# A four-layer graph network in one list schedule: the planner gets the SBUF port of VectorE and GpSimd as a resource, finer costs, and new ranks

## The chip, the cores and the metric

The kernel runs on one core of a Trainium2 chip. The metric is the device time of one execution in microseconds (us), and the figure for a kernel is the median over its runs. The engines are called by the names of the profile: PE (TensorE), DVE (VectorE), ACT (ScalarE), POOL (GpSimd) and SP (SyncE, which here only issues DMAs). PEld is PE's weight load.

## The reference

The input `x` holds 128 batches of 128 nodes by 512 features, all in f32; `adj` is one 128x128 matrix. Four layers follow each other, and each is `x = layernorm(x + layer(x))`:

```
layer 0:  y = adj @ x[b];  y @ weight + bias
layer 1:  h = x @ W;  e = leaky_relu(s1[:,None] + s2[None,:]) * adj   (s1, s2 = h @ a1, h @ a2)
          elu(softmax(e) @ h + beta * h)
layer 2:  A = adj @ x,  C = adj @ x + b;  max over nodes of relu(A + (C - A))
layer 3:  8-head attention masked where adj == 0, projection,  o + layernorm(o) * gamma + beta
```

Batches are independent of each other. The order of the work is free as long as each batch goes through its layers in turn.

## The kernel before

**Tiling.** A batch is one 128x512 tile. Batches are taken in groups: 31 groups of four and, at the end, two groups of two (`PAIRS`). Layer 0 and layer 1 multiply two batches at a time, layer 3's Q, K and V a group at a time. These products use a scheme with seven block multiplications where the plain one has eight (`seven`, `pair_product`, `section`). The scheme needs four differences of activation blocks for each product (`differences`, line 908, on POOL) and, once, sums of weight blocks (`sums`, line 587, on POOL). The first `DIRECT` batches go through layer 0 with the plain product instead (`product`, line 362, and `mixed`, line 370). A batch that is not direct is mixed by line 389, transposed by DVE (line 392), and reordered through a scratch tensor in DRAM.

**Storage.** All activations live in one SBUF arena of 105 units, cut into classes of slots (`CAPS`, `SIZES`). PSUM has eight banks. Activations that wait for the end of layer 3 are spilled to DRAM and fetched again, except for the last `KEPT` batches.

**The order.** Nothing orders the engines but the order in which instructions are issued on each of them, and semaphores between them. That order is made when the program is built, by a list scheduler, the class `Plan`. Every batch, group and side task is a Python generator (a chain). It yields requests such as `use("DVE", 0.7, "t")`: engine, planned duration in us, slots that it needs. `Plan.at` gives the earliest time at which a request can start by the plan's own clock; `Plan.run` always takes the request with the earliest start, then the smaller order (`follow`, `urgent`, other), then the smaller rank, and lets its chain emit the instructions. A planned duration is multiplied by a factor for its engine (`SLACK`: DVE 1.05, ACT 1.1, POOL 1.0, SP 1.1), and the time from the end to the next step is `HANDOFF`, or, for a DMA, its own figure times `LATE`. The plan's times only decide the order. On the chip, every instruction starts when its engine and its semaphores let it.

In the plan before, one request often covers several DVE instructions. The three passes at lines 733, 737 and 739 and the reduction at 745 are one request of 2.2 us, lines 1415 and 1419 are one of 2.0 us, and the two passes of line 1151 are one of 1.7 us.

**Ranks.** A batch's rank is its number (the last 20 get four less, `early`). Constants shift it: `SECTION` for Q, K and V, `PROJ` for what follows attention, `SOFT` for the softmax, `SOON` for each of the last six groups, `SUMS0` and `SUMS3` for the weight sums. `RUN` makes a batch wait until the group that many groups earlier has its layer-3 input. `tiled` weaves the score matmuls (line 1049) of a group with the attention products (line 1070) of the one before it; for the last `APART` groups the attention products are chains of their own (`attend`). For the last `WHOLE` batches the softmax of layer 3 is taken whole (lines 1252 to 1258: an addition on DVE, one exponential on ACT, a sum on DVE); for the others, ACT takes eight exponentials with their row sums (line 1262).

**Lines that the steps touch.** DVE with two inputs in SBUF: 733, 737, 739, 757 (layer 1's attention), 1151 (its logits), 1175 and 1192 (elu), 1270 (softmax scale), 1415 and 1419 (layer 3's norm). DVE with an input in PSUM: 800, 804, 806, 818 (sums of the seven products), 1143, 1240. POOL: 309 (the power -0.5 of a variance), 355 (`pool_add`), 587, 908. ACT: 343 to 349 (layer norm), 812 (copies out of PSUM), 1311.

Of the kernel before, what the change touches and what calls it, by code (L numbers as in the profile page):

```python
# [18 lines left out]
G = 4  # L19
APART = 7  # L20
FIRST = 0
PAIRS = 2
SOON = (-2, 0, -2, 6, 12, 18)
WHOLE = 4
KEPT = 7
ATTENDS = 2
RUN = 7
SEVEN0 = 1
SUMS2 = 1
SUMS0 = 2  # L30
SUMS3 = 12
# [4 lines left out]
PLAIN = 4  # L36
GUESTS = 12
STICK = 0.4
CLOSE = 2900
SOFT = 4  # L40
PROJ = -5
SECTION = 14
PACE = 0
# [14 lines left out]
LAST, AHEAD = 20, 4  # L58
DIRECT = 12
LATER = 3  # L60
LANDED = 2.2
LATE = 1.3
HANDOFF = {"PE": 0.2, "DVE": 0.13, "ACT": 0.16, "POOL": 0.09, "SP": 0.05}
DVE_ = 1.05
ACT_ = 1.1
POOL_ = 1.0
SP_ = 1.1
SLACK = {"PE": 1.0, "DVE": DVE_, "ACT": ACT_, "POOL": POOL_, "SP": SP_}
BORDERS = 0.1
MARGIN = 0.5  # L70
LAND, ROW_LAND = 2.8, 0.0053
# [13 lines left out]
class Plan:  # L85
# [16 lines left out]

    def use(self, engine, work, take=None, late=None, urgent=False, follow=False, kind=""):
# [7 lines left out]
        return engine, work * SLACK[engine], names, late, 0 if follow else 1 if urgent else 2, kind  # L111

# [48 lines left out]
    def at(self, r):  # L161
        engine, _, take, _, order, _ = r["want"]
        spare = MARGIN if r["ready"] < CLOSE else 0.7
        early = min(spare, r["ready"] / 20) if engine == "PE" and order else 0.0
        t = max(r["ready"] + early, self.free.get(engine, 0.0))
        names = take()
        wanted = {}
        for name in names:
            n = SIZES.get(name, 0)
            wanted[n] = wanted.get(n, 0) + 1  # L170
        for n, count in wanted.items():
            free = self.blocks[n] if n else self.banks
            t = max(t, min(free) if count == 1 else sorted(free)[count - 1])
        for name in set(names) & set(CAPS):
            t = max(t, sorted(self.caps[name])[names.count(name) - 1])
        return t
# [29 lines left out]
    def run(self):  # L206
        while self.requests:
            t, _, _, n = min(
                (self.at(r) + self.border(r["want"]), r["want"][4], r["rank"], n)
                for n, r in enumerate(self.requests)  # L210
            )
            assert t < float("inf"), "the chains wait for each other"
            r = self.requests.pop(n)
            t = self.at(r)
            engine, work, take, late, _, kind = r["want"]
            if engine == "PE":
                work += BORDERS * (kind != self.kind)
                self.kind = kind
            self.free[engine] = t + work
            self.now = r["ready"] = t + work + late  # L220
            got = self.claim(take(), t)
            self.step(r, got[0] if len(got) == 1 else got)

# [8 lines left out]
def gnn_stack_kernel(  # L232
# [74 lines left out]
    def root(ve, rstd, follow=False):  # L307
        yield use("POOL", 0.62, urgent=True, follow=follow)
        nc.gpsimd.tensor_tensor(rstd, ve, neghalf, op=ALU.pow)  # L309
        return rstd  # L310
# [39 lines left out]

    def pool_add(dst, other, event, after=None, work=1.38):
        if after:
            yield after
        yield use("POOL", work)
        nc.gpsimd.tensor_tensor(dst, dst, other, op=ALU.add)  # L355
        done(event)
# [223 lines left out]
    def sums(s):  # L580

        for out, a, b, op in (
            (S1, S3, A22, ALU.add), (S2, S1, A11, ALU.subtract),
            (S3, A11, S3, ALU.subtract), (S4, A12, S2, ALU.subtract),
        ):
            yield use("POOL", 1.4)
            nc.gpsimd.tensor_tensor(weight(s, out), weight(s, a), weight(s, b), op=op)
# [26 lines left out]
    def logit_rows(a_sb, slot):  # L614

        yield w1_in
        wa = const.tile([P, K, 2], F32, name="wa")
        for s in range(2):
            for k in range(K):
                b_s = yield use("DVE", 0.7, "t")  # L620
# [88 lines left out]
    def attention1(gr, h):  # L709
# [21 lines left out]
        )  # L731
        be = yield use("DVE", 2.2, "u", urgent=True)
        nc.vector.tensor_tensor(
            z, z, s[:, 2 * h : 2 * h + 2, 0:1].to_broadcast([P, 2, P]), op=ALU.add
        )
        e = buf(be, 2, P)
        nc.vector.scalar_tensor_tensor(e, z, ALPHA, z, op0=ALU.mult, op1=ALU.max)
        give(bz)
        nc.vector.tensor_tensor(
            e, e, adj_cols.rearrange("p c r -> p (c r)")[:, None, :].to_broadcast([P, 2, P]),  # L740
            op=ALU.mult,
        )
        n = small.tile([P, 3, 2], F32, name="logits", bufs=4)
        nmx, sums, rs = n[:, 0], n[:, 1], n[:, 2]
        nc.vector.tensor_reduce(nmx, e, axis=AX.X, op=ALU.max, negate=True)
        yield use("ACT", 0.77)
        for i in range(2):
# [3 lines left out]
            )  # L751
        bt = yield use("DVE", 1.6, "u")
        nc.vector.reciprocal(rs, sums)
        et = buf(bt, Q, 2, S)
        for i in range(2):

            nc.vector.scalar_tensor_tensor(
                e[:, i, :], e[:, i, :], rs[:, i : i + 1], beta_id, op0=ALU.mult, op1=ALU.add
            )
            nc.vector.transpose(et[:, :, i, :], e[:, i, :].rearrange("p (c r) -> p c r", c=Q))  # L760
# [12 lines left out]
    def gather(gr):  # L773
# [16 lines left out]
        gr.xT[2] = buf(gr.slot["xT", 2], 1, 2, n)  # L790
        yield from differences(gr.block, gr.have, gr.used, 0.18 + 0.58 * gr.half, gr.first)

# [106 lines left out]
    def differences(blocks, have, used, time, rank):  # L899

        for out, a, b, when, t in (
            (T3, B22, B12, None, T3), (T1, B12, B11, None, T1),
            (B11, B22, T1, used[B11], T2), (B21, B21, B11, used[B21], T4),
        ):
            if when:
                yield when
            yield use("POOL", time, urgent=True)
            nc.gpsimd.tensor_tensor(blocks(out), blocks(a), blocks(b), op=ALU.subtract)  # L908
            done(have[t])

    def pair_product(rank, s, ready, blocks, release, out, finished, differed=None, into=None):
# [23 lines left out]

        plan.start(differences(blocks, have, used, 0.78, rank), rank)

# [161 lines left out]
    def batch(i):  # L1099
# [47 lines left out]
        yield wa_ready  # L1147
        b_s = yield use("DVE", 1.7, "t")
        unread = buf(b_s, D)
        for j in range(2):  # L1150
            nc.vector.scalar_tensor_tensor(  # L1151
                unread, xb, 1.0, wa_rows[:, j, :], op0=ALU.mult, op1=ALU.mult,
# [7 lines left out]
        if SEVEN1:  # L1160
# [12 lines left out]
            unread = be  # L1173
            yield use("DVE", 0.75, urgent=True)
            nc.vector.scalar_tensor_tensor(xb, ex, 0.0, xb, op0=ALU.max, op1=ALU.add)
            yield use("ACT", 0.52, urgent=True)
            nc.scalar.activation(ex, ex, AF.Exp)
        else:
# [10 lines left out]
            unread = bp  # L1189
        yield use("DVE", 0.77)  # L1190
        total = row_sums()
# [58 lines left out]
        if i >= NB - WHOLE:  # L1250
            yield use("DVE", 1.4)
            nc.vector.tensor_tensor(
# [6 lines left out]
        else:  # L1259
            for j in range(H):  # L1260
# [4 lines left out]
                )  # L1265
        yield use("DVE", 0.1 if SCALED == H else 0.1 + 1.45 * (1 - SCALED / H))
        rs = small.tile([P, H], F32, name="rs3")
# [139 lines left out]
    def normed(i, o, release, fetched):  # L1407
# [20 lines left out]
    def last(i, oT, v, release, biased):  # L1428
# [22 lines left out]
        for h, columns in enumerate(halves):  # L1451
# [7 lines left out]
            give(bp)  # L1459
            plan.start(pool_add(xb[:, columns], o[:, columns], added, biased, 0.9), i)  # L1460
        yield use("DVE", 0.32, follow=True)
# [3 lines left out]
        rooted, _ = beside(root(ve, rstd, follow=True), i)  # L1465
        b_t1 = yield use("DVE", 0.66, "t", follow=True)
        t1 = buf(b_t1, D)
# [4 lines left out]
        yield added  # L1472
        yield use("DVE", 1.8, follow=True)
        nc.vector.scalar_tensor_tensor(xb, t1, rstd, xb, op0=ALU.mult, op1=ALU.add)
# [54 lines left out]
```

## Time and profile before

| | us |
|---|---|
| median of 3 runs | 2994.31 |
| lowest and highest | 2992.17, 2995.53 |
| the profiled execution | 2995.11 |
| its span, first to last instruction | 2993.1 |
| PE busy | 2941.6 |
| DVE busy | 2457.0 |
| ACT busy | 2402.7 |
| POOL busy | 1873.3 |

The mean granted PE clock over the span is 0.996. Durations in what follows come from the profiled execution, whose own time lies 0.8 us above the median. "Busy" is the time in which an engine has an instruction in flight. A view of groups gives, for each line and shape, the count, the summed busy time and the mean duration, and the idle time of the engine just ahead of them with what ended it. A view of waits gives the waiting engine and line, the engine and line that it waited for, then the sum, the number of waits and the longest.

### The profile page before, as it was taken

What the parts mean: (1) busy time and instruction counts of PE and PEld (TensorE: products, weight loads), DVE (VectorE), ACT (ScalarE), POOL (GpSimd) and SP (SyncE); (2) the same over time, 40 slices, a digit from 0 to 9 for tenths busy, and PEclk for the clock granted to TensorE, in tenths of its full rate; (3) what the DMA queues carried; (4) which work ended last, traced back from release to release, by engine and by line L of the source; (5) the groups of instructions that cost most, each with busy time, mean ns of one, the idle gap of its engine ahead of it and who ended that gap; (6) DMA issues with size and microseconds to landing.
All of it is one profiled execution on the core that took longest, in us unless ns stands there. A gap on an engine that the chain in (4) does not pass through costs nothing. (4 is left out here: it accounts for less than half of the span.)

```text
span 2993.1 us, 55166 instructions
## 1 busy us (share of the span) xinstructions
PE 2941.6 (98%) x16503; PEld 2481.8 (83%) x16503; DVE 2457.0 (82%) x5775; ACT 2402.7 (80%) x7368; POOL 1873.3 (63%) x2049
## 2 busy tenths in 40 slices
PE   8999999999999999999999999999999999999997
PEld 5788788888888888888888888888888888888886
DVE  7977888877888888888878788887898877878778
ACT  4789688787978888888787887887888878778885
POOL 7954657555656756565755676665676647565555
PEclk9999999999999999999999999999999999999999
DMA  6535546544655655554654646555655545454443
GB/s 208 137 88 148 160 130 164 141 129 115 179 140 148 164 141 156 149 151 128 163 138 113 184 135 162 147 140 135 166 152 144 156 134 153 114 140 124 116 141 127
DMA packets 884105, 430.84 MB, mean 144 GB/s; under 512 B 572128, under 2 KB 785760, under 8 KB 883808
## 3 DMA queue, kind: packets, MB, share of 16 engines
q1 hardware_dynamic: 865376, 393.75, 48.7%
q10 hardware_dynamic: 18432, 33.56, 3.0%
q8 instruction: 133, 2.18, 0.3%
q14 instruction: 164, 1.34, 0.1%
HBM read 222.36 MB, written 204.80 MB: 143 GB/s over the span
## 5 line engine op out<-in xcount | busy, mean ns | idle before, releaser
L908 POOL TENSOR_TENSOR arena<-arena 128x256 f32<-128x256 f32 (+1 forms) x868 | 763.0, 888 | 325.1 <-PE ps L921 82.3
L309 POOL TENSOR_TENSOR sums<-sums,neghalf 128x1 f32<-128x1 f32 x511 | 322.4, 633 | 511.5 <-ACT sums L345 504.5
L921 PE MATMUL ps<-wsum_sb,arena 128*128 128x256 f32 x2208 | 547.1, 381 | 13.5 <-POOL arena L908 8.0
L921 PEld LDWEIGHTS ps<-wsum_sb,arena 128*128 128x128 f32 x2208 | 415.6, 191 | 95.3 <-POOL arena L908 14.7
L921 PE MATMUL ps<-w_sb,arena 128*128 128x256 f32 x1952 | 482.2, 381 | 5.0 <-DVE arena L806 3.5
L970 PE MATMUL ps<-arena,wqkv_sb 128*128 128x256 f32 (+1 forms) x2112 | 480.8, 373 | 0.0
L812 ACT COPY arena<-ps 128x256 f32<-128x256 f32 (+1 forms) x892 | 338.3, 395 | 158.7 <-PE ps L921 91.0
L970 PEld LDWEIGHTS ps<-arena,wqkv_sb 128*128 128x128 f32 x2112 | 393.5, 191 | 67.3 <-issue 16.2
L343 ACT ACTIVATE arena<-arena,sums 128x512 f32<-128x512 f32 x499 | 357.0, 716 | 114.5 <-DVE sums L338 94.1
L921 PEld LDWEIGHTS ps<-w_sb,arena 128*128 128x128 f32 x1952 | 371.0, 191 | 79.9 <-issue 20.2
L349 ACT ACTIVATE arena<-arena,sums 128x512 f32<-128x512 f32 x511 | 415.9, 814 | 17.1
L806 DVE TENSOR_TENSOR arena<-ps,arena 128x256 f32<-128x256 f32 (+1 forms) x669 | 291.7, 452 | 133.5 <-ACT arena L812 57.0
L1262 ACT ACTIVATE arena<-arena,nmx 128x128 f32<-128x128 f32 x992 | 388.3, 394 | 10.2 <-DVE nmx L1248 10.2
L970 PE MATMUL ps<-arena,wsum_sb 128*128 128x256 f32 (+1 forms) x1584 | 356.6, 374 | 5.6 <-POOL arena L908 3.7
L970 PEld LDWEIGHTS ps<-arena,wsum_sb 128*128 128x128 f32 x1584 | 293.8, 191 | 57.6 <-issue 11.0
L1276 ACT ACTIVATE arena<-arena,rs 128x128 f32<-128x128 f32 x768 | 281.1, 395 | 12.4 <-DVE rs L1268 8.2
L355 POOL TENSOR_TENSOR arena<-arena,beta_sb 128x512 f32<-128x512 f32 x128 | 170.3, 1334 | 141.3 <-DVE arena L1223 130.1
L1151 DVE SCALAR_TENSOR_TENSOR arena<-arena,wa_rows 128x512 f32<-128x512 f32 x256 | 224.7, 879 | 21.7 <-ACT arena L349 17.0
L970 PE MATMUL ps<-wqkv_sb,arena 128*128 128x256 f32 x1024 | 242.0, 380 | 0.0
L921 PE MATMUL ps<-wproj_sb,arena 128*128 128x256 f32 x992 | 240.5, 384 | 0.2
L970 PEld LDWEIGHTS ps<-wqkv_sb,arena 128*128 128x128 f32 x1024 | 194.4, 190 | 31.5 <-issue 4.7
L355 POOL TENSOR_TENSOR arena<-arena,bproj_sb 128x512 f32<-128x512 f32 x124 | 173.8, 1411 | 65.1 <-ACT arena L812 54.2
(120 smaller groups left out, 5490.9 us busy)
## 6 DMA issues: line engine op xcount, KB each, us to landing
p_d<-arena SPq DMA_DIRECT2D x256, 256.0 KB
arena<-p_d SPq DMA_DIRECT2D x128, 512.0 KB
x_d<-arena SPq DMA_DIRECT2D x244, 256.0 KB
arena<-x_d SPq DMA_DIRECT2D x976, 64.0 KB
arena<-in_x SPq DMA_DIRECT2D x127, 256.0 KB
out<-arena ACTq DMA_DIRECT2D x127, 256.0 KB
x_s<-arena SPq DMA_DIRECT2D x121, 256.0 KB
arena<-x_s SPq DMA_DIRECT2D x121, 256.0 KB
```

The lines of the kernel that those rows point to most:

```text
L309: nc.gpsimd.tensor_tensor(rstd, ve, neghalf, op=ALU.pow)
L343: nc.scalar.activation(buf_or_bank(unread), xb, AF.Square, bias=nm, accum_out=squares)
L349: nc.scalar.activation(xb, xb, AF.Identity, bias=nmr, scale=rstd)
L355: nc.gpsimd.tensor_tensor(dst, dst, other, op=ALU.add)
L806: nc.vector.tensor_tensor(c, a, c, op=ALU.add)
L812: nc.scalar.copy(c, a)
L908: nc.gpsimd.tensor_tensor(blocks(out), blocks(a), blocks(b), op=ALU.subtract)
L921: nc.tensor.matmul(p, t[:, k], w[:, k, :], start=first and k == 0, stop=final and k == 1, skip_group_check=True,)
L970: nc.tensor.matmul(to, lhs, rhs, start=first and j == 0 and k == 0, stop=final and k == 1, skip_group_check=True,)
L1151: nc.vector.scalar_tensor_tensor(unread, xb, 1.0, wa_rows[:, j, :], op0=ALU.mult, op1=ALU.mult, accum_out=gr.s[:, b, j : j + 1],)
L1262: nc.scalar.activation(pr[:, j, :], pr[:, j, :], AF.Exp, bias=nmx[:, j : j + 1], accum_out=sums[:, j : j + 1],)
L1276: nc.scalar.activation(pr[:, j, :], pr[:, j, :], AF.Identity, scale=rs[:, j : j + 1])
```

## The change

No instruction is given another form. The change does four things.

1. `use` takes `port=`: the planned time for which a request holds the SBUF port that DVE and POOL share. A request with a port starts only when the port is free in the plan. POOL's additions and differences hold it for their whole planned time; its power at line 309 waits for it and does not hold it (`port=0.0`). DVE's passes with two SBUF inputs hold it.
2. Requests that covered several two-input DVE passes are split, one request for each pass.
3. Planned durations are new (POOL's addition 1.38 to 1.23, its power 0.62 to 0.51, a difference 0.78 to 0.69), and so are the factors for DVE and ACT, and `LATE`.
4. Constants of rank and staging are new. Three of them change which instructions are issued: `DIRECT` (two more batches take the plain product), `WHOLE` (no batch takes the softmax whole) and `KEPT` (one more batch is spilled).

```diff
-APART = 7
+APART = 4
-SOON = (-2, 0, -2, 6, 12, 18)
-WHOLE = 4
-KEPT = 7
+SOON = (-2, 2, -4, 10, 6, 18)
+WHOLE = 0
+KEPT = 6
-RUN = 7
+RUN = 6
-SUMS0 = 2
+SUMS0 = 0
-GUESTS = 12
-STICK = 0.4
+GUESTS = 16
+STICK = 0.6
-SOFT = 4
-PROJ = -5
-SECTION = 14
+SOFT = 6
+PROJ = -6
+SECTION = 12
-DIRECT = 12
+DIRECT = 14
-LATE = 1.3
+LATE = 1.6
-DVE_ = 1.05
-ACT_ = 1.1
+DVE_ = 1.0
+ACT_ = 1.02
+PORT = 1.0
...
     def at(self, r):
...
         t = max(r["ready"] + early, self.free.get(engine, 0.0))
+        if port is not None:
+            t = max(t, self.free.get("port", 0.0))
...
+    def issue(self, r):
...
+        self.free[engine] = t + work
+        if port:
+            self.free["port"] = t + port * PORT
...
     def root(ve, rstd, follow=False):
-        yield use("POOL", 0.62, urgent=True, follow=follow)
+        yield use("POOL", 0.51, urgent=True, follow=follow, port=0.0)
...
-    def pool_add(dst, other, event, after=None, work=1.38):
+    def pool_add(dst, other, event, after=None, work=1.23):
...
-        yield use("POOL", work)
+        yield use("POOL", work, port=work)
...
-        be = yield use("DVE", 2.2, "u", urgent=True)
+        yield use("DVE", 0.35, urgent=True, port=0.33)
         nc.vector.tensor_tensor(
             z, z, s[:, 2 * h : 2 * h + 2, 0:1].to_broadcast([P, 2, P]), op=ALU.add
         )
+        be = yield use("DVE", 0.35, "u", urgent=True, port=0.33)
...
-            yield use("POOL", time, urgent=True)
+            yield use("POOL", time, urgent=True, port=time)
...
-        b_s = yield use("DVE", 1.7, "t")
-        unread = buf(b_s, D)
         for j in range(2):
+            got = yield use("DVE", 0.68, lambda: () if j else ("t",), port=0.6)
+            b_s = b_s if j else got
+            unread = buf(b_s, D)
...
-        b_t1 = yield use("DVE", 2.0, "t")
+        b_t1 = yield use("DVE", 0.66, "t", port=0.64)
...
+        yield use("DVE", 0.74, port=0.64)
         total = row_sums()
```

The passes at lines 757, 1175, 1192, 1252 and 1270 and the weight sums get their port in the same way.

More of the change, by code (lines that the diff above doesn't have):

```diff
@@ L101, in __init__, with use @@
         self.now, self.kind = 0.0, ""
-    def use(self, engine, work, take=None, late=None, urgent=False, follow=False, kind=""):
+    def use(self, engine, work, take=None, late=None, urgent=False, follow=False, kind="", port=None):
         names = take if callable(take) else lambda: (take,) if take else ()
         late = HANDOFF[engine] if late is None else late * LATE
-        return engine, work * SLACK[engine], names, late, 0 if follow else 1 if urgent else 2, kind
+        order = 0 if follow else 1 if urgent else 2
+        return engine, work * SLACK[engine], names, late, order, kind, port
     def start(self, chain, rank):
@@ L161, in at @@
     def at(self, r):
-        engine, _, take, _, order, _ = r["want"]
+        engine, _, take, _, order, _, port = r["want"]
         spare = MARGIN if r["ready"] < CLOSE else 0.7
@@ L212, in run @@
             assert t < float("inf"), "the chains wait for each other"
[L213 to L222, printed above, removed]
+            self.issue(self.requests.pop(n))
+    def issue(self, r):
+        t = self.at(r)
+        engine, work, take, late, _, kind, port = r["want"]
+        if engine == "PE":
+            work += BORDERS * (kind != self.kind)
+            self.kind = kind
+        self.free[engine] = t + work
+        if port:
+            self.free["port"] = t + port * PORT
+        self.now = r["ready"] = t + work + late
+        got = self.claim(take(), t)
+        self.step(r, got[0] if len(got) == 1 else got)
     def border(self, want):
@@ L585, in sums @@
         ):
-            yield use("POOL", 1.4)
+            yield use("POOL", 1.23, port=1.23)
             nc.gpsimd.tensor_tensor(weight(s, out), weight(s, a), weight(s, b), op=op)
@@ L619, in logit_rows @@
             for k in range(K):
-                b_s = yield use("DVE", 0.7, "t")
+                b_s = yield use("DVE", 0.61, "t", port=0.6)
                 nc.vector.scalar_tensor_tensor(
@@ L738, in attention1 @@
         give(bz)
+        yield use("DVE", 0.35, urgent=True, port=0.33)
         nc.vector.tensor_tensor(
@@ L742, in attention1 @@
         )
+        yield use("DVE", 0.36, urgent=True)
         n = small.tile([P, 3, 2], F32, name="logits", bufs=4)
@@ L751, in attention1 @@
             )
-        bt = yield use("DVE", 1.6, "u")
+        bt = yield use("DVE", 0.12, "u")
         nc.vector.reciprocal(rs, sums)
@@ L755, in attention1 @@
         for i in range(2):
+            yield use("DVE", 0.59, port=0.25)
             nc.vector.scalar_tensor_tensor(
@@ L790, in gather @@
         gr.xT[2] = buf(gr.slot["xT", 2], 1, 2, n)
-        yield from differences(gr.block, gr.have, gr.used, 0.18 + 0.58 * gr.half, gr.first)
+        yield from differences(gr.block, gr.have, gr.used, 0.15 + 0.54 * gr.half, gr.first)
     def seven(rank, bx, wide, time, multiply, parts, finished, have, home, housed, slow=0.0, into=None, scale=None):
@@ L934, in parts @@
             yield t, out[j][:, i * D // 2 : (i + 1) * D // 2]
-        plan.start(differences(blocks, have, used, 0.78, rank), rank)
+        plan.start(differences(blocks, have, used, 0.69, rank), rank)
         def home(j):
@@ L1173, in batch @@
             unread = be
-            yield use("DVE", 0.75, urgent=True)
+            yield use("DVE", 0.6, urgent=True, port=0.6)
             nc.vector.scalar_tensor_tensor(xb, ex, 0.0, xb, op0=ALU.max, op1=ALU.add)
@@ L1189, in batch @@
             unread = bp
-        yield use("DVE", 0.77)
+        yield use("DVE", 0.61, port=0.55)
         total = row_sums()
@@ L1250, in batch @@
         if i >= NB - WHOLE:
-            yield use("DVE", 1.4)
+            yield use("DVE", 1.13, port=1.1)
             nc.vector.tensor_tensor(
@@ L1265, in batch @@
                 )
-        yield use("DVE", 0.1 if SCALED == H else 0.1 + 1.45 * (1 - SCALED / H))
+        short = (1.0 - SCALED / H) * 1.13
+        yield use("DVE", 0.18 + short + 0.11 * (SCALED < H), port=0.18 + short if short else None)
         rs = small.tile([P, H], F32, name="rs3")
@@ L1459, in last @@
             give(bp)
-            plan.start(pool_add(xb[:, columns], o[:, columns], added, biased, 0.9), i)
+            plan.start(pool_add(xb[:, columns], o[:, columns], added, biased, 0.71), i)
         yield use("DVE", 0.32, follow=True)
@@ L1465, in last @@
         rooted, _ = beside(root(ve, rstd, follow=True), i)
-        b_t1 = yield use("DVE", 0.66, "t", follow=True)
+        b_t1 = yield use("DVE", 0.66, "t", follow=True, port=0.64)
         t1 = buf(b_t1, D)
@@ L1472, in last @@
         yield added
-        yield use("DVE", 1.8, follow=True)
+        yield use("DVE", 1.8, follow=True, port=0.66)
         nc.vector.scalar_tensor_tensor(xb, t1, rstd, xb, op0=ALU.mult, op1=ALU.add)
```

## The prediction

> **What bounds the kernel now.** I read the page's busy line first, then a table of busy time by stage, then TensorE's waits, then single instructions.
>
> The page's first line says that TensorE (PE) has a matmul in flight 98% of the span:
>
> ```profile
> PE 2941.6 (98%) x16503; PEld 2481.8 (83%) x16503; DVE 2457.0 (82%) x5775; ACT 2402.7 (80%) x7368; POOL 1873.3 (63%) x2049
> ```
>
> So at most 2993.1 - 2941.6 = 51.5 us are idle on PE by the records, and the change adds or removes almost no matmul. The forecast is about those 51.5 us. The table of stages says where they lie (columns: stage, length, then busy time and count of PE, weight load, DVE, ACT, POOL; granted PE clock, DMA share, GB/s):
>
> ```profile
> 0.00:100.00 100.00, 86.72 (x342) 55.43 (x343) 82.90 (x171) 47.35 (x121) 73.59 (x71) 0.97 0.55 179
> 100.00:300.00 200.00, 199.78 (x1064) 168.53 (x1063) 160.04 (x398) 175.28 (x530) 123.40 (x137) 1.00 0.50 129
> 300.00:850.00 550.00, 539.63 (x3029) 457.33 (x3028) 451.54 (x1056) 440.29 (x1366) 343.57 (x377) 1.00 0.53 147
> 850.00:2550.00 1700.00, 1694.91 (x9536) 1442.06 (x9536) 1402.54 (x3361) 1396.17 (x4281) 1080.00 (x1189) 1.00 0.54 147
> 2550.00:2950.00 400.00, 393.35 (x2418) 341.29 (x2416) 325.10 (x717) 320.78 (x1017) 225.19 (x249) 1.00 0.45 127
> 2950.00:2994.00 44.00, 27.23 (x125) 17.18 (x123) 34.86 (x77) 22.83 (x56) 27.53 (x29) 0.85 0.34 113
> ```
>
> Length less PE busy gives the idle time: **head 13.3, then 0.2, then 10.4 in 300 to 850, 5.1 in the long middle, 6.7 in 2550 to 2950, tail 15.9** (43.1 us of span less 27.2). The middle is at 99.7%: nothing can be won there. What PE waited for, whole span:
>
> ```profile
> PE ps L921 <- POOL arena L908: 8.0, 7, 3.0
> PE ps L370 <- DMA arena<-e_d: 4.2, 3, 2.6
> PE ps L970 <- POOL arena L908: 3.7, 4, 2.4
> PE ps L362 <- ACT arena L1311: 3.5, 2, 2.8
> PE ps L921 <- DVE arena L806: 3.5, 1, 3.5
> ```
>
> The largest is GpSimd's block differences (L908, 8.0 + 3.7 us): an operation that reads SBUF. The 3.5 us before L806 is one gap in the head, and the timeline there shows its cause:
>
> ```profile
> 83.83 0.76 DVE L1151 SCALAR_TENSOR_TENSOR arena<-arena,wa_rows 128x512 f32<-128x512 f32 x1
> 84.00 1.71 POOL L587 TENSOR_TENSOR wsum_sb<-wproj_sb 128x512 f32<-128x512 f32 x1
> ...
> 84.63 1.62 DVE L1151 SCALAR_TENSOR_TENSOR arena<-arena,wa_rows 128x512 f32<-128x512 f32 x1
> 85.79 1.59 POOL L587 TENSOR_TENSOR wsum_sb<-wsum_sb,wproj_sb 128x512 f32<-128x512 f32 x1
> ...
> 86.19 0.74 DVE L806 TENSOR_TENSOR arena<-ps,arena 128x256 f32<-128x256 f32 x2
> 86.75 2.04 PE L921 MATMUL ps<-w_sb,arena 128*128 128x256 f32 x4 [3.51 <-DVE arena L806]
> ```
>
> The second L1151 takes 1.62 us, and it ends just after POOL's L587 does; the eviction L806 stands behind it on DVE, and PE behind L806. The median L1151 takes 692 ns, the shortest 648, the longest 1781. L806, with one input in PSUM, never exceeds 693 in either of its two sizes.
>
> **What the Trainium skill says.** "SBUF — State Buffer", section "Who interferes with whom": a VectorE instruction with two SBUF inputs contends with a GpSimd instruction that reads SBUF, one of them holds the port for its whole length, and the other blocks; with one SBUF input VectorE does not contend. The trace agrees (1.62 against 692 ns). "Perfetto Trace Analysis", section "Identifying the Most-Contended Engine": matmul busy share is a poor measure of the distance to the roof. It agrees: in steady stretches 16 matmuls of 128x256 start within 3.45 us, 216 ns each, where a record is 381 ns long. "TensorE: Matmul & The Clock Gate", section "What's actually happening": a PE that has been idle runs slower. It agrees: eight L362 matmuls took 3.70 us at 2963.05 and 5.40 us at 2970.61, after 2.84 us of idle, and the granted clock of the tail is 0.85.
>
> PE's pure work at steady pace: 10,656 matmuls of 256 columns x 0.216, 608 of 512 x 0.431, 1,142 of 128 x 0.11 (32 of L370 in 3.57 us on the chain of waits), 4,096 of the tiled ones (L1049, L1070; 64 in 3.64 us) x 0.057 make about 2922 us. So nearer 71 us than 51.5 are open, and about 20 of them can hardly go (first data, last batch's chain).
>
> **The change, part by part.**
>
> *What collisions cost now.* For each two-input pass: (mean less its undisturbed time) x count. L1151 (879-692)x256 = 48 us; L1175 (855-687)x128 = 22; L1192 (893-684)x128 = 27; L1415 (1035-690)x127 = 44; L1419 (1098-750)x127 = 44; L1270 (723-488)x128 = 30; L733, L737, L739 together 46; L757 18: **279 us of DVE's 2457.** On POOL, L309 57, L355 51, L908 62: **170 of 1873.** This is delay of engines that are not the bound; it costs only where PE waits.
>
> *The port in the plan.* No instruction is changed and nothing on the chip enforces the port: only the order of each engine's queue moves. The old plan charged L1415 with L1419 2.0 x 1.05 = 2.1 us, near their mean sum 2.13, so it knew the average and not when. The new one charges 0.66 + 0.74 and holds the port. The gaps that it can close are those whose last waits end at L908 or at DVE. I take half of the 10.4 us in 300 to 850 (-5), 2 of 6.7 in 2550 to 2950, 1 of 5.1 in the middle. Bounds: all 22.2 gone at best; as much added at worst.
>
> *Other costs of the planner.* ACT 1.1 to 1.02: square, accumulator and L345 planned 1.03 take 1.03 in the trace, so 1.02 is nearer. LATE 1.3 to 1.6: e_d's two transfers, planned 1.9 x 1.3 = 2.5 and 2.5 x 1.3 = 3.25, take 3.18 and 3.69 us on the chain at 2780 to 2788; the new plan says 3.0 and 4.0. At stake are the 4.2 us of L370's waits. Counted within the figures above.
>
> *DIRECT 12 to 14.* Batches 12 and 13 use the plain product. PE: +2 x (8 x 0.11 + 8 x 0.431) = +8.7 us, less 2 x 0.86 (L389) and 28 x 0.216 (L921) = 7.8: **+0.9 us.** DVE: +2 x 0.76 (L1143), less 2 x 0.71 (L392), 3 x 0.41 (L818), 4 x 0.49 (L800): -3.1. POOL: four L908 fewer, -3.2. ACT: two L381 copies, +1.2. SP: two scratch writes and eight reads fewer. w0 keeps two of the ten qk slots somewhat longer; QKV's first matmul is at 157 us, the last direct product at 68, so I charge nothing, 2 us if that cover is gone. DVE and POOL are what the head lacks: between 80 and 90 us they are busy 9.86 and 9.92 of 10, with 24 L587 sums (some 36 us) due in the head. SUMS0 and GUESTS 12 to 16 move w0's sums and x loads ahead; those loads go through SP, ahead of the scratch reads queued behind them. Head together: -4 + 0.9 = **-3** (bounds -8 and +6).
>
> *WHOLE 4 to 0.* The last four batches lose L1252 (1.32 us) and L1258 (1.20) on DVE, and swap one 1.05 us exponential for eight of about 0.38 on ACT: latency 3.6 to 3.0 us a batch, DVE -10, ACT +8. In 2930 to 2950 DVE is busy 8.7 to 9.9 of 10, ACT 6.3 to 6.6: it goes the right way. KEPT 7 to 6: one spill and one fetch more on SP (256 KB each), well ahead of use. APART 7 to 4 weaves three more groups' attends between the score matmuls, and SOON, PROJ, SECTION, SOFT, RUN shift ranks: of unknown sign. In the tail, L1415 takes 1.75 and L1419 1.58 us at 2965 to 2969 beside POOL's L355, and the ACT copy that the last product needs comes behind them; without that 2 us go. Tail: **-2** (bounds -8 and +8).
>
> Sum: -5 -1 -2 -3 -2 = -13 us on a profiled execution of 2995.1 (span 2993.1 and 2.0 around it), which lies 0.8 above the median of the runs. That makes 2982.1 us; I say **2982**.
>
> **Rivals.** (A) *The forecast*: 2972 to 2988. Chance 0.50.
>
> (B) *A larger gain.* The collision delays fall by half, head and tail each lose 6, 300 to 850 and 2550 to 2950 nearly all of their 17: about 28 us, 2966. For it: the head's and tail's stalls do stand behind collided passes. Against: the head also waits for data, the tail for the last batch's own chain. Chance 0.16.
>
> (C) *The order changes, the time doesn't.* Chip and plan drift apart by more than a port slot (0.6 us), so collisions fall where they may, PE stays at 98%, and the rest is a serial chain at both ends. 2993, within 0.2%. For it: no instruction holds the port. Chance 0.16.
>
> (D) *Slower: port exclusion makes the differences late.* The plan now starts L908 only when no two-input pass holds the port, so it sits up to 0.6 us later in POOL's order, behind adds (L355, 1.27 us) and roots (L309), and a section of PE waits. The two L908 rows total 11.7 us over 11 waits; 868 / 4 = 217 sets of four pass. If one set in six costs PE a 0.6 us wait, that is 22 us, less 8 won at the ends: +14, 3008. It decides from 13 us of added waits, where it outweighs the gain. For it: L908 already leads the waits. Against: POOL is 63% busy. Chance 0.18.
>
> **How the numbers follow.** 0.2% (6 us) is about what a measurement of this kernel can tell from no change. Faster by more: A and B, 0.66; within it: C, 0.16; slower: D, 0.18. The range reaches from near B's figure, 2965, to 3001, which leaves out some 0.1 on either side; the likeliest case's own range is 2972 to 2988.
>
> **What would show it.** Right: mean L1151, L1415 and L1419 fall (below 830, 950 and 1000 ns), DVE's busy time falls by over 60 us, PE's busy stays near 2941, idle in 300 to 850 falls to about 5 us, the 3.5 us gap before L921 at 86 us is gone, L1252 and L1258 vanish, L362 counts 16 more. Wrong: means as before (C), or L908 above 20 us among PE's waits (D), or new idle in the middle.

## The result, and the profile after

| | before | after |
|---|---|---|
| median of the runs, us | 2994.64 | 2963.67 |
| lowest and highest, us | 2992.17, 2995.53 | 2962.32, 2965.09 |
| the profiled execution, us | 2995.11 | 2962.69 |
| its span, us | 2993.1 | 2960.9 |
| mean granted PE clock | 0.996 | 0.998 |

The ratio is 0.9898 (95% interval 0.9881 to 0.9915), so the changed kernel is 31 us faster, where 12 were forecast. The time lies 1.3 us below the range.

The page's busy line of the kernel after:

```profile
PE 2932.6 (99%) x16503; PEld 2476.2 (84%) x16503; DVE 2334.8 (79%) x5758; ACT 2390.1 (81%) x7430; POOL 1832.6 (62%) x2045
```

DVE is busy 122 us less, POOL 41, PE 9.0, with the same number of matmuls. The table of stages, with the columns of the one before; the last row is again the last 43 us:

```profile
0.00:100.00 100.00, 98.40 (x387) 62.33 (x387) 70.19 (x163) 54.83 (x130) 80.59 (x82) 1.00 0.65 208
100.00:300.00 200.00, 193.45 (x960) 161.02 (x961) 162.66 (x444) 178.32 (x507) 119.57 (x135) 0.99 0.44 117
300.00:850.00 550.00, 548.10 (x3164) 468.59 (x3163) 434.98 (x1038) 441.86 (x1420) 334.50 (x372) 1.00 0.54 148
850.00:2550.00 1700.00, 1696.91 (x9594) 1448.75 (x9594) 1356.88 (x3377) 1388.20 (x4333) 1066.57 (x1194) 1.00 0.55 148
2550.00:2918.00 368.00, 366.94 (x2260) 317.06 (x2260) 277.79 (x662) 301.24 (x971) 201.08 (x231) 1.00 0.46 128
2918.00:2961.00 43.00, 28.85 (x144) 18.46 (x142) 32.33 (x78) 25.62 (x73) 30.25 (x33) 0.90 0.45 141
```

PE's idle time falls from 13.3 to 1.6 us in the head, but 6.6 come up in 100 to 300, where 0.2 were. It falls from 10.4 to 1.9 in 300 to 850, from 5.1 to 3.1 in the middle, and from 22.5 to 15.1 after 2550, of which the last 43 us still hold 14.1. Together 51.5 becomes 28.3. The stages are cut by time, not by work: at 300 us the kernel after has issued 1347 matmuls, the one before 1406, so the idle times of a stage belong to partly different work. What PE waited for, whole span:

```profile
PE ps L1214 <- ACT arena L357: 4.6, 5, 1.7
PE ps L932 <- ACT arena L823: 3.4, 3, 2.0
PE ps L932 <- POOL arena L919: 3.0, 2, 1.7
...
PE ps L981 <- POOL arena L919: 1.3, 3, 0.8
```

Line numbers have moved: 908 is now 919, 921 is 932, 970 is 981, 1151 is 1163, 1415 and 1419 are 1428 and 1433. POOL's differences, 11.7 us before, now cost PE 4.3. The gap of 3.51 us at 86 us is gone. PE's timeline there has no wait:

```profile
83.39 1.02 PE L397 MATMUL ps<-arena,adjT 128*128 128x512 f32 x2
84.25 1.03 PE L932 MATMUL ps<-wsum_sb,arena 128*128 128x256 f32 x4
85.11 1.89 PE L932 MATMUL ps<-w_sb,arena 128*128 128x256 f32 x8
86.84 1.03 PE L932 MATMUL ps<-wsum_sb,arena 128*128 128x256 f32 x4
```

The groups of the five large passes with two SBUF inputs (count, then busy us and mean ns). First two of them in the kernel before, then the kernel after:

```profile
L1151 DVE SCALAR_TENSOR_TENSOR arena<-arena,wa_rows 128x512 f32<-128x512 f32 x256 | 224.7, 879 | 21.7 <-ACT arena L349 17.0
L1419 DVE SCALAR_TENSOR_TENSOR arena<-arena,n 128x512 f32<-128x512 f32 x127 | 139.5, 1098 | 15.4 <-POOL n L309 2.2 <-DVE arena L1415 0.5
```

```profile
L1163 DVE SCALAR_TENSOR_TENSOR arena<-arena,wa_rows 128x512 f32<-128x512 f32 x256 | 208.4, 822 | 32.2 <-ACT arena L357 28.6 <-POOL arena L919 1.7 <-ACT arena L351 1.1
L1428 DVE SCALAR_TENSOR_TENSOR arena<-arena,n,gamma_sb 128x512 f32<-128x512 f32 x127 | 123.7, 975 | 1.3 <-DMA x_d<-arena 1.3
L1433 DVE SCALAR_TENSOR_TENSOR arena<-arena,n 128x512 f32<-128x512 f32 x127 | 117.6, 928 | 1.2
L1187 DVE SCALAR_TENSOR_TENSOR arena<-arena 128x512 f32<-128x512 f32 x128 | 107.2, 840 | 21.2 <-ACT arena L823 19.9
L1204 DVE SCALAR_TENSOR_TENSOR arena<-arena 128x512 f32<-128x512 f32 x128 | 96.2, 757 | 7.6 <-ACT arena L1189 7.5
```

All means fell (879, 1035, 1098, 855 and 893 before), but none is undisturbed. With the undisturbed times of the prediction, the excess of these and the smaller two-input passes is 174 us after 279. One of those times is too short: 690 ns for L1415, whose shortest instance takes 702 and whose median after is 748. With 748 the two sums are 166 and 272. Either way, more than half of DVE's collision delay is still there.

### The profile page after: what moved, and what is told of

It reads as the page before. It is cut to its first block, busy times and chain, and to the rows that moved or that the text cites. A ratio compares the mean times of both kernels' runs of the same rounds, so it can differ in the third digit from the quotient of the medians.

```text
span 2960.9 us, 55267 instructions
## 1 busy us (share of the span) xinstructions
PE 2932.6 (99%) x16503; PEld 2476.2 (84%) x16503; DVE 2334.8 (79%) x5758; ACT 2390.1 (81%) x7430; POOL 1832.6 (62%) x2045
## 5 line engine op out<-in xcount | busy, mean ns | idle before, releaser
L919 POOL TENSOR_TENSOR arena<-arena 128x256 f32<-128x256 f32 (+1 forms) x864 | 746.2, 870 | 387.8 <-PE ps L932 101.6
L317 POOL TENSOR_TENSOR sums<-sums,neghalf 128x1 f32<-128x1 f32 x511 | 329.2, 645 | 530.7 <-ACT sums L353 523.5
L823 ACT COPY arena<-ps 128x256 f32<-128x256 f32 (+1 forms) x892 | 336.2, 394 | 159.3 <-PE ps L932 78.2
L981 PEld LDWEIGHTS ps<-arena,wqkv_sb 128*128 128x128 f32 x2112 | 392.1, 190 | 65.1 <-issue 13.2
L357 ACT ACTIVATE arena<-arena,sums 128x512 f32<-128x512 f32 x511 | 415.8, 814 | 17.1
L1274 ACT ACTIVATE arena<-arena,nmx 128x128 f32<-128x128 f32 x1024 | 402.9, 400 | 2.9 <-DVE nmx L1260 2.7
L1163 DVE SCALAR_TENSOR_TENSOR arena<-arena,wa_rows 128x512 f32<-128x512 f32 x256 | 208.4, 822 | 32.2 <-ACT arena L357 28.6
L932 PEld LDWEIGHTS ps<-wproj_sb,arena 128*128 128x128 f32 x992 | 186.1, 190 | 31.5 <-issue 3.7
```

What stands on the lines that cost most here:

```text
L357: nc.scalar.activation(xb, xb, AF.Identity, bias=nmr, scale=rstd)
L823: nc.scalar.copy(c, a)
L932: nc.tensor.matmul(p, t[:, k], w[:, k, :], start=first and k == 0, stop=final and k == 1, skip_group_check=True,)
L981: nc.tensor.matmul(to, lhs, rhs, start=first and j == 0 and k == 0, stop=final and k == 1, skip_group_check=True,)
L1163: nc.vector.scalar_tensor_tensor(unread, xb, 1.0, wa_rows[:, j, :], op0=ALU.mult, op1=ALU.mult, accum_out=gr.s[:, b, j : j + 1],)
L1274: nc.scalar.activation(pr[:, j, :], pr[:, j, :], AF.Exp, bias=nmx[:, j : j + 1], accum_out=sums[:, j : j + 1],)
```

## The experiments

**What they are to tell apart.** Three theories were set up after the result. *P*: keeping the passes apart is the gain by itself. *R*: the port makes the plan's clock true, and the gain comes from choosing constants by a true clock. *S*: the constants that change which instructions are issued (`DIRECT`, `WHOLE`, `KEPT`; here "the structure") are the gain. Theories that only some runs bear on (D, L) are stated with them. Each ratio is to runs of the kernel before made beside that experiment, whose median lay between 2994.9 and 2997.1 us. Differences between experiments are therefore taken from the ratios; a ratio is known to about 0.15%, a difference of two to about 0.2%, which is 6 us.

"The plan's clock ends at" is the largest value in `Plan.free` once all chains are done. The program computes it while it is built; it is no time of the chip. It is given beside each measurement because its distance to the measured span is the test of R.

**1. Port, new durations, old constants** (`e1`).

```diff
-APART = 4
-SOON = (-2, 2, -4, 10, 6, 18)
-WHOLE = 0
...
-DIRECT = 14
+APART = 7
+SOON = (-2, 0, -2, 6, 12, 18)
+WHOLE = 4
...
+DIRECT = 12
```

> The changed kernel with the twelve constants of the kernel before (APART, SOON, WHOLE, KEPT, RUN, SUMS0, GUESTS, STICK, SOFT, PROJ, SECTION, DIRECT); port, split requests and new durations stay. Theory P (a plan that knows when passes collide is the gain by itself): 2965 to 2975, near the changed kernel. Theory R (the port only makes the plan's clock true, so that constants chosen by that clock pay on the chip; with constants chosen for another clock there is no gain): the plan's own clock ends at 2995 here against 2957 for the changed kernel, so about 2995 to 3005. Theory S (the gain is the structural edits, DIRECT and WHOLE): about 2985 to 2994.

Measured: 3002.78 us, ratio to the kernel before 1.002 (1.0012 to 1.0027). Span 3001.5, clock 2995. Its busy line:

```profile
PE 2945.5 (98%) x16503; PEld 2482.9 (83%) x16503; DVE 2354.1 (78%) x5775; ACT 2373.8 (79%) x7368; POOL 1826.5 (61%) x2049
```

DVE is busy 103 us less than before, and the kernel is no faster; the time lies in R's 2995 to 3005. P is refuted as an account of the gain: fewer collisions alone don't shorten the kernel before. PE is idle 56.0 us here, 51.5 before.

**2. Old plan, new constants** (`e2`): the twelve constants the other way round, in the kernel before.

> The kernel before with the twelve new constants alone; no port, old durations and factors. P: no gain, 2990 or more. R: the constants fit another clock, so no gain: 2990 to 3040. S: DIRECT and WHOLE are in, so 2965 to 2980. In the two-input passes the mean durations stay as before (L1151's row near 880 ns) under P and R.

Measured: 3037.85 us, ratio 1.0134 (1.0118 to 1.015); span 3035.7, clock 3007. The constants are bad for the plan they weren't chosen for, and S in its simple form is refuted as well: `DIRECT` and `WHOLE` are in, and 40 us are lost. R's 2990 to 3040 is met, but L1151's mean is 924 ns, not the 880 or so of the kernel before.

**3. Port held 5% longer** (`e3`).

```diff
-PORT = 1.0
+PORT = 1.05
```

> The changed kernel with PORT 1.05 instead of 1.0: every hold of the port 5% longer in the plan, all else the same. P: within 5 us of the changed kernel, 2959 to 2969. R: the plan's own clock ends at 3032 instead of 2957, 75 us later, and if that clock is true the chip follows: 3020 to 3045.

Measured: 3028.44 us, ratio 1.0104 (1.0086 to 1.0122); span 3025.6, clock 3032. The order that the plan makes is so sensitive that 5% on one resource costs the chip some 62 us, and the clock had said 75; R's 3020 to 3045 is met. PE's waits after 2550 us show what this order did:

```profile
PE ps L1081 <- DMA arena<-p_d: 22.4, 3, 14.1
PE ps L397 <- DMA arena<-in_x: 7.5, 2, 6.9
PE ps L370 <- ACT arena L1324: 6.7, 1, 6.7
```

Here PE waits for attention's transposed probabilities and for an input that was loaded late, not for a collided pass. DVE's busy time is 2312.1 us, lower than in the changed kernel. That is a second strike against P.

**4. No collision in the plan, old constants** (`e4`): as the first, with `PORT = 0.0`.

> As the first run of this set, but with PORT 0: split requests and undisturbed durations, no collision in the plan at all, constants of the kernel before. Its plan's clock ends at 2952. P: collisions unplanned, slower than the first run by 15 to 30 us, about 2990 to 3000. R: the clock is false by some 40 us, 2985 to 3000, and the first run, whose clock says 2995, is no better. The difference of clock and chip is the test: near 5 us with the port, 35 to 50 without.

Measured: 3098.46 us, ratio 1.0338 (1.0321 to 1.0354); span 3097.2, clock 2952. P and R had both put it at 3000 at most, and the clock is 145 us early, not 35 to 50. The kernel before had collisions in its durations as averages; with undisturbed durations and no port nothing accounts for them. The middle of this kernel:

```profile
850.00:2550.00 1700.00, 1652.34 (x9175) 1384.31 (x9175) 1346.15 (x3252) 1336.85 (x4166) 1035.26 (x1147) 1.00 0.53 143
```

PE is idle 47.7 us there, 3.1 in the changed kernel. No wait dominates (the longest sums, over the whole span, are 16.3 us for L823's copies, 15.5 for L357, 14.6 for L919): no single cause stands out in this view. Against `e1`, which differs in the port alone, 96 us are lost: with these constants and undisturbed durations the port is needed, though against averaged ones it brings nothing until constants are chosen by it.

**5. and 6. The structure undone piece by piece** (`e5`, `e6`), ranks left as they are.

```diff
-DIRECT = 14
+DIRECT = 12
```
```diff
-WHOLE = 0
+WHOLE = 4
```

> The changed kernel with DIRECT 12 again. The plan's clock ends at 2967 against 2957. Theory R (the clock is true, so the chip follows it): 2964 to 2982. Theory S (DIRECT is worth a fixed amount, the head's stall at 80 to 90 us comes back): PE's idle time in 0 to 100 us goes from 1.6 back to 8 or more, and the total is 2970 to 2980. Under R the loss may lie anywhere in the span.

Measured: 2976.40 us, ratio to before 0.9934 (0.9919 to 0.9949); span 2974.0, clock 2967.

> The changed kernel with WHOLE 4 again: the last four batches take their softmax whole. The plan's clock ends at 2961 against 2957. R: 2960 to 2974. S (the tail gains from it): 2966 to 2972, with the loss after 2850 us. If DVE's ten added us count for nothing: 2959 to 2966.

Measured: 2969.86 us, ratio to before 0.9911 (0.9896 to 0.9926); span 2969.0, clock 2961. By the ratios they lose 11 and 4 us against the changed kernel, and the second is not clear of the noise. Both times lie in R's range and in S's, so they do not tell the two apart. With `DIRECT` 12, PE's idle time before 100 us is 5.3 instead of 1.6, not the 8 that S asked for. Another 3.5 us come in the middle, where no direct batch is. With `WHOLE` 4, the plan's order is that of the changed kernel up to 2889 us of the plan's clock, so what it loses can lie only after that, as S says. The last stage is 8 us longer, but it also holds 26 more matmuls (170 against 144):

```profile
2850.00:2918.00 68.00, 68.00 (x591) 61.89 (x589) 57.61 (x116) 55.51 (x181) 32.71 (x39) 1.00 0.38 110
2918.00:2969.00 51.00, 34.02 (x170) 21.83 (x168) 39.65 (x89) 26.90 (x67) 32.62 (x34) 0.84 0.40 129
```

**7. Half the port** (`e7`): `PORT = 0.5`, new constants.

> The changed kernel with PORT 0.5: each pass holds the port half as long in the plan. The plan's clock ends at 2970. R: the clock is false again, by something between the 6 us with the whole port and the 145 with none, so 2995 to 3060, and the sum of DVE and POOL busy time rises by 40 to 100 us. Rival (any sign of the port is enough, since a start is never planned inside another's first half): 2970 to 2985.

Measured: 3068.64 us, ratio 1.0238 (1.0221 to 1.0255); span 3069.7, clock 2970. The clock is 100 us early. DVE and POOL together are busy 109 us more than in the changed kernel. R had the direction, but both figures lie beyond its ranges (3060 and 100). The rival is refuted: any sign of the port isn't enough.

**8. The old factor on landing times** (`e8`): `LATE = 1.3`.

> The changed kernel with LATE 1.3, the old factor on a DMA's landing time. The plan's clock ends at 2967. If the landing times matter (theory D): the clock is too early for each of the reads that PE waits for, the chip ends 15 to 35 us after the clock, 2984 to 3004, and PE waits for DMAs by over 15 us in total. If only the port matters (theory R in its narrow form): within 8 us of the clock, 2964 to 2978.

Measured: 2979.99 us, ratio to before 0.9944 (0.993 to 0.9959); span 2977.5, clock 2967. The chip is 10.5 us behind the clock, between what D and the narrow R had said, and the time is in neither range. PE's waits for DMAs are not among its largest (e_d 1.8 us). The factor matters little for the clock's truth; the rest of the loss is in the order, as the clock says.

**9. to 11. Constants chosen anew by each clock** (`f1`, `f2`, `f3`). Changes of up to three constants at a time were tried, and what ended earlier by the plan's clock was kept.

```diff
-SOON = (-2, 2, -4, 10, 6, 18)
-WHOLE = 0
-STICK = 0.6
+SOON = (-2, 4, -4, 14, 6, 19)
+WHOLE = 1
+STICK = 0.4
...
```

> The changed kernel with constants chosen anew by trying changes of up to three of them at a time and keeping what ends earlier by the plan's own clock (with the port): APART 5, SOON (-2, 4, -4, 14, 6, 19), WHOLE 1, STICK 0.4, SUMS3 13, ATTENDS 1. The clock ends at 2948 instead of 2957. Theory R (a true clock can be used to choose): 2950 to 2960, faster than the changed kernel. Rival L (which order is fast on the chip is luck, the clock tells no more than some tens of us): 2965 to 3010.

> A second choice by the same clock from another chain of trials: APART 5, SOON (-2, 0, -4, 12, 6, 18), WHOLE 3, SUMS0 -2, STICK 0.8, SOFT 10, SCALED 8, LATER 2. The clock ends at 2948. R: 2950 to 2960. L: 2965 to 3010.

Measured: 2962.12 us (0.9892, 0.9877 to 0.9907) and 2961.99 us (0.9892, 0.9875 to 0.9908); spans 2958.8 and 2959.4, clocks 2948 both. R's number is missed: the clock promised 9 us more than the changed kernel, and the chip gave less than 2, which these runs can't tell from nothing. The rival L's range is missed too, and its reason fails: two other chains of trials end within 2 us of the changed kernel. Below some 10 us the clock says no more. Both kernels also move instructions: `WHOLE` is 1 in `f1` and 3 in `f2`, and with `SCALED` 8 `f2` leaves no scaling pass of line 1283 on DVE. Their times don't show it.

> The kernel before, with constants chosen in the same way by its own clock, without the port: RUN 5, GUESTS 14, PROJ -6, SUMS3 10, LATER 5, ATTENDS 1. That clock ends at 2945 instead of 2951. R: the clock is 30 to 45 us early and what it gains is its own error, so 2978 to 3000, no clear gain over the kernel before. Rival (choosing harder is what gained, with any clock): 2960 to 2985.

Measured: 2989.77 us, ratio 0.998 (0.9972 to 0.9989); span 2985.6, clock 2945. The old clock ends earlier here than the clock with the port in any kernel, and the chip is 40 us behind it, as it was in the kernel before (42). R's range is met, its reason is not: what the old clock gained was not its own error. It promised 6 us against the kernel before, and the ratio gives 6. The rival's range is missed.

**12. The old factors** (`f4`): `DVE_ = 1.05`, `ACT_ = 1.1`.

> The changed kernel with the old factors for DVE (1.05) and ACT (1.1). The plan's clock ends at 3057, 100 us later. If the plan's order is what is bad there: 3030 to 3060, with the chip somewhat ahead of the clock, since its passes are shorter than planned. If it is only the clock that is late and the order is as good: 2960 to 2990.

Measured: 3038.94 us, ratio 1.0146 (1.0131 to 1.0161); span 3038.3, clock 3057. The order is bad on the chip too, and the chip is 18 us ahead of the clock.

**13. and 14. Structure and clock crossed, each with ranks of its own** (`g1`, `g2`). Since the single undos kept ranks chosen for another structure, these two test S with ranks of their own.

```diff
 # g1: the changed kernel
-DIRECT = 14
-WHOLE = 0
-KEPT = 6
+DIRECT = 12
+WHOLE = 4
+KEPT = 7
...
 # g2: the kernel before
-DIRECT = 12
-WHOLE = 4
-KEPT = 7
+DIRECT = 14
+WHOLE = 0
+KEPT = 6
...
```

> The changed kernel with DIRECT 12, WHOLE 4 and KEPT 7 as before, and the ranks chosen anew by the clock with the port (APART 5, SOON (-2, 2, -4, 9, 6, 18), GUESTS 15, SOFT 7, PROJ -4, SECTION 13, SUMS3 19). The clock ends at 2953. Theory R: 2957 to 2969, level with the changed kernel. Theory S (the structural constants are worth 10 us and more): 2974 to 2986.

> The kernel before with DIRECT 14, WHOLE 0 and KEPT 6, and the ranks chosen anew by its own clock, without the port (APART 5, SOON (-2, 0, -2, 6, 8, 23), RUN 6, SUMS0 4, GUESTS 14, STICK 0.6, SOFT 6, PROJ -2, LATER 2). The clock ends at 2943. R: 29 to 45 us behind the clock, 2973 to 2990. S: 2960 to 2972.

Measured: `g1` 2970.08 us (0.9915, 0.9898 to 0.9931), `g2` 2981.15 us (0.995, 0.9935 to 0.9964). Ranks chosen anew by its own clock in each cell, as ratios to the kernel before:

| | old structure | new structure |
|---|---|---|
| old clock | 0.998 (`f3`) | 0.995 (`g2`) |
| clock with the port | 0.9915 (`g1`) | 0.9892 (`f1`, `f2`, with `WHOLE` 1 and 3); the changed kernel 0.9898 |

Read down a column, the clock is worth 0.65 and 0.58%, 17 to 20 us. Read along a row, the structure is worth 0.30 and 0.23%, 7 to 9 us. Each difference is known to about 6 us, so the clock's share is clear and the structure's hardly is. With `WHOLE` at 0, 1 and 3 in that last cell, its times differ by nothing measurable, so what the structure gives is not shown to come from `WHOLE`. Within the noise the two add up. What is left, 0.2% from the kernel before to `f3`, is choosing harder with the same clock. "Clock" here means the port with the split requests, new durations and factors, and `LATE`, together; no run chose ranks anew for one of these alone. `g2` lies in R's 2973 to 2990 and not in S's range; `g1` missed R's 2957 to 2969 by 1 us, and S's figure by 4.

The same stages of `g2` and of `g1`, old clock first:

```profile
0.00:100.00 100.00, 90.80 (x372) 58.77 (x373) 81.15 (x169) 47.04 (x118) 74.91 (x70) 0.97 0.49 169
850.00:2550.00 1700.00, 1692.12 (x9533) 1438.61 (x9532) 1407.94 (x3368) 1394.60 (x4297) 1085.70 (x1188) 1.00 0.54 148
```
```profile
0.00:100.00 100.00, 95.52 (x380) 61.85 (x381) 74.29 (x171) 47.13 (x115) 80.66 (x82) 1.00 0.68 217
850.00:2550.00 1700.00, 1693.60 (x9549) 1439.14 (x9548) 1353.88 (x3361) 1384.27 (x4310) 1060.04 (x1189) 1.00 0.54 147
```

With the port in the clock, PE does 4.7 us more in the head (95.5 of 100 against 90.8), at full granted clock where the other gets 0.97. In the middle they are at 99.5 and 99.6%, though DVE is 54 us less busy in `g1`.

**The clock against the chip**, all kernels (us; "chip" is the profiled span):

| port in the plan | kernel | clock | chip | chip less clock |
|---|---|---|---|---|
| whole | after, `e1`, `e5`, `e6` | 2957, 2995, 2967, 2961 | 2960.9, 3001.5, 2974.0, 2969.0 | 4, 6, 7, 8 |
| whole | `f1`, `f2`, `g1` | 2948, 2948, 2953 | 2958.8, 2959.4, 2968.3 | 11, 12, 15 |
| whole, `LATE` 1.3 | `e8` | 2967 | 2977.5 | 11 |
| whole, durations or hold too long | `e3`, `f4` | 3032, 3057 | 3025.6, 3038.3 | -6, -18 |
| none, averaged durations | before, `e2`, `f3`, `g2` | 2951, 3007, 2945, 2943 | 2993.1, 3035.7, 2985.6, 2980.4 | 42, 29, 40, 38 |
| half | `e7` | 2970 | 3069.7 | 100 |
| none, undisturbed durations | `e4` | 2952 | 3097.2 | 145 |

With the whole port the chip follows the clock within 18 us over a range of 110. Averages leave it 29 to 42 us early. Sorted by the clock of their own plan, the kernels without the port would all have looked better than the changed one, but for `e2`. The changed kernel's plan ends 6 us later than the one before, so its whole gain is in what the chip adds to the plan's end: 4 us instead of 42.

That the old clock is early is not by itself what spoils the choice. Among the four kernels with averaged durations, the clock (2943, 2945, 2951, 3007) gives the chip's own order (2980.4, 2985.6, 2993.1, 3035.7). What the runs show is that the best kernels found with that clock stay 17 to 20 us above those found with the other. A rival stays open: no run raised the averages until the plan's end met the chip's and then chose ranks by that clock, so it is not shown that the port as a resource with a start and an end is what does it.

## Why the prediction was wrong

The direction was right and the waits named were the right ones; the size was not. By the terms of its sum (us; the measured column is the change of PE's idle time, from the tables of stages):

| term | forecast | measured |
|---|---|---|
| head, idle (0 to 300) | -4 | -5.3 |
| 300 to 850 | -5 | -8.5 |
| middle | -1 | -2.0 |
| 2550 to the end (-2 and -2) | -4 | -7.4 |
| PE busy | +0.9 | -9.0 |
| sum | -13 | -32 |

**The step that failed first** is the pricing of the port as a term of its own: "I take half of the 10.4 us in 300 to 850 (-5), 2 of 6.7 in 2550 to 2950, 1 of 5.1 in the middle", with ranks "of unknown sign" beside it, so at nothing. The runs show that neither part gains alone. The port with the old constants (`e1`) makes the kernel 0.2% slower, the new constants in the old plan (`e2`) 1.3% slower, and the two together 1.0% faster. That the port's term came out with the right sign is therefore luck. Avoided collisions, which I took as the cause, are no measure of the gain: `e1` has DVE busy 2354.1 and is slower than before.

The fractions were wrong too. Before, 7.0 us of PE's waits in 300 to 850 and 6.2 in 2550 to 2950 ended at L908 or DVE, the kind that the prediction said can be closed. After, 0.2 of these 13.2 are left, where 7 were to go. But a stage that is cleared is not the mark of the port. `f3`, with ranks chosen by the old clock, clears 300 to 850 as well (10.4 to 1.9) and pays in the middle (5.1 to 11.0):

```profile
300.00:850.00 550.00, 548.11 (x3080) 467.11 (x3079) 454.14 (x1079) 459.04 (x1417) 355.32 (x390) 1.00 0.56 155
850.00:2550.00 1700.00, 1689.04 (x9510) 1430.91 (x9509) 1397.84 (x3339) 1393.58 (x4299) 1067.69 (x1179) 1.00 0.53 146
```

Over the whole span PE is idle 42 us in `f3` and in `g2`, and 28 to 34 in the changed kernel, `f1`, `f2` and `g1`.

**The second is PE's busy time.** I had worked out that "nearer 71 us than 51.5 are open", from the pace of the matmuls, and then summed only idle time. PE busy fell by 9.0 us, where +0.9 was forecast: half of the 19 us by which the sum is off. (The 71 was itself too small. The 10,656 matmuls "of 256 columns" hold 224 of L970 that have 128; with the prediction's own paces the pure work is about 2899 us, not 2922, and some 94 us are open.) The granted clock went from 0.97 to 1.00 in the head and from 0.85 to 0.90 in the last 43 us, in line with what the prediction takes from the Trainium skill, "TensorE: Matmul & The Clock Gate", section "What's actually happening": PE idles less, and its granted clock is higher. Over the span the clock rose from 0.996 to 0.998, which on 2941.6 us makes about 6 us, an estimate from these figures. How much of the 9 us is clock, and how much the modelled ends of matmuls ahead of gaps that are gone, was not separated.

**Structure.** With `DIRECT` the forecast reason is borne out: in `e5`, with `DIRECT` 12, DVE is busy 73.4 us in the head instead of 70.2, and PE idle 5.3 instead of 1.6. For `WHOLE` it is not shown, as `f1` and `f2` are as fast with 1 and 3. "Head together -3" and "Tail -2" make 5 us against the 7 to 9 of the crossed runs, no difference at a noise of 6.

**The rivals.** B had the size (2966) and the stages: it gave 300 to 850 and 2550 to 2950 nearly all of their 17 us, and 14.1 went. Its reason, collision delays halved, doesn't hold: DVE's excess is 174 of 279 us, and the tail lost 1.8 us, not 6. C's mechanism, chip and plan drifting apart, fits the kernel before (42 us) better than the one after (4). D was not seen; PE's waits for L908 fell from 11.7 to 4.3 us. Of the signs named, L1151 (822 ns) and L1419 (928) were met, L1415 (975 against 950) not; DVE's busy time fell by more than 60, and PE's did not stay near 2941. Idle in 300 to 850 fell further than the 5 us named, and new idle came up in 100 to 300, of which 3.0 us are behind the differences and 2.5 behind ACT's L357. Where the prediction rested on the Trainium skill, "SBUF — State Buffer", section "Who interferes with whom", the trace after agrees: L1163's median is 685 ns (692 before), and the longest of its instances still take 1.8 us (one L1428 took 2.8).

## What to carry to other kernels

When a planner orders the queues, put its own end beside the chip's span before tuning ranks. Here the old plan's end was 40 us early, and ranks chosen by it gained 6 us; ranks chosen by a plan that the chip follows within some 15 us were worth 17 to 20 us more. Don't price the plan and the ranks apart: the ranks that fit one plan did not fit the other, and either part alone made this kernel slower. A resource that two engines share can go into the plan as a resource with a start and an end, since an average in the durations says how much is lost and not when; that a better average wouldn't do as well is not shown. Judge a schedule change by PE's idle time and pace over all stages together, not by one stage, and not by the busy time of engines that aren't the bound.

## What was not expected of the hardware

POOL's power at line 317 (309 before) works on 128x1 and takes 548 ns at the median in the changed kernel, yet up to 1143: it waits for the port as the large passes do. Of its 196 instances over 600 ns, 195 overlap a DVE pass with two SBUF inputs. Here one starts beside L1187, which ends at 1522.67, and ends 0.41 us after that:

```profile
1521.31 1.36 DVE L1187 SCALAR_TENSOR_TENSOR arena<-arena 128x512 f32<-128x512 f32 x1
1522.08 1.00 POOL L317 TENSOR_TENSOR sums<-sums,neghalf 128x1 f32<-128x1 f32 x1
```

Over its 640 instances that is 62 us (means 645 and 643 ns less 548), more than the 44 us by which the 740 small differences (791 less 732 ns) are delayed:

```profile
L317 POOL TENSOR_TENSOR sums<-sums,neghalf 128x1 f32<-128x1 f32 x511 | 329.2, 645 | 530.7 <-ACT sums L353 523.5 <-DMA arena<-x_d 2.9 <-DMA arena<-in_x 1.0
L317 POOL TENSOR_TENSOR n<-n,neghalf 128x1 f32<-128x1 f32 x129 | 82.8, 643 | 27.9 <-DVE n L312 18.6 <-DVE sums L346 9.3
```

And the chip repeats a given order closely (2962.3 to 2965.1 us in the changed kernel), while a change of 5% in one planned figure (`e3`) moved the time by some 62.
